# A graph layer on one core: maxima of turned tiles and clearing of sums moved to ScalarE, the additions at segment ends moved away from their products, 75 columns and 16 single lines a chunk

## The chip, the core and the metric

The kernel runs on one core of a Trainium2 chip. The metric is the device time of one execution in microseconds (us). A core has five engines with a queue of instructions each: TensorE (PE), VectorE (DVE), ScalarE (ACT), GpSimd (POOL) and SyncE (SP). They run side by side and wait for each other by semaphores only.

## The reference

There are 12,500 nodes of 48 numbers and 400,000 edges of 32 numbers, sorted by their target `dst`; the sources `src` are in no order.

```python
h = jnp.maximum(_layernorm(x, axis=-1), 0.0)
tmp = jnp.concatenate([h[dst], h[src], edge_attr], axis=1)
msg = jax.nn.relu(tmp @ W1 + b1) @ W2 + b2
return x + jax.ops.segment_sum(msg, dst, num_segments=12500)
```

## The kernel before

A first stage of about 100 us (`node_tables`) makes two tables of the nodes: `tab_a` (h times the target's part of W1, with b1) and `tab_b` (h times the source's part), both in device memory with one line of 128 numbers a node, and `bt`, which is `tab_b` turned, with a column a node, in SBUF.

Then `windows` walks through the edges. A chunk `c` is 1,024 edges, in eight tiles of 128; there are 391. As the edges are sorted, the targets of a chunk lie in a window of 80 nodes. For each chunk:

- SP loads 80 lines of `tab_a` (`rhs`), the edges' attributes and targets (`lhs`, `row`). DVE makes `lhs` one-hot rows out of the targets (L463) and `hot`, the same as columns (L469). PE multiplies `lhs` with `rhs` into `pre` (L481): targets' part and attributes' part in one product of a tile.
- The sources' part of a tile comes in one of three ways. POOL fetches 128 lines of `tab_b` with an indirect DMA into `gb` (L452), and DVE adds them to `pre` (L517). Or the tile is "turned": DVE and ACT copy 128 single columns of `bt` into a tile `gt`, one instruction a column (L393), and PE turns and adds that to `pre` (L491). Or it is a "single" tile: SP fetches 128 lines, one DMA a line (L425), into `gr`, and DVE adds them (L515).
- DVE takes the maximum with zero: of gathered and single tiles in place in `hid` (L530), of turned tiles from `pre` to `hid` (L532).
- PE multiplies `hid` with `hot` into `p_g` (L541), and counts with `ones` (L546); DVE adds `p_g` to `seg` (L560).

A table `PARTS` says how many columns are copied per chunk: 71 by DVE in four parts, 80 by ACT in five. With 151 columns per chunk 458 tiles are turned (`tiles_of`: 389 * 151 // 128), with 12 single lines 36 tiles are single (389 * 12 // 128), and 3125 - 458 - 36 = 2631 are left for POOL. Each part's node numbers are loaded into the engine's registers first (`numbers`, L358, a TENSOR_LOAD in the engine's own queue).

Twelve chunks are a segment, kept in one of two buffers `seg` of 1,024 nodes. After the last chunk of a segment DVE clears the other buffer (L576) and copies what overlaps (L578). In the next two iterations PE multiplies half of `seg` each with W2 and b2 into `p_f` (L586, L587), DVE adds it to `xseg` (L588), and SP stores.

The order of the work is written by hand (`manual_schedule`): in iteration `c` stand `prepare(c)`, `before(c - 1)`, `fold(c - 2)`, `turned(c - 1)`, then the segment's sum, `gathered(c - 1)`, `hidden(c - 1)` and `add(c - 2)`, with DVE's parts of columns in between and ACT's at the end. PE's last product into `pre` waits for the fetched lines. POOL may run up to seven chunks ahead (`gp` has eight buffers; `paced` ties a fetch to DVE's work of seven chunks earlier). ACT writes ahead into the `gt` buffers, of which there are five.

Of the kernel before, what the change touches and what calls it, by code (L numbers as in the profile page):

```python
# [8 lines left out]
F32 = mybir.dt.float32  # L9
I32 = mybir.dt.int32  # L10
# [6 lines left out]
P = 128  # L17
# [5 lines left out]
T = 8  # L23
# [12 lines left out]
BLK = 512  # L36
STORE = 2
NOUT = NPAD + L
# [16 lines left out]
PARTS = (  # L55
    (True, 0, 19, 1),
    (True, 19, 20, 20),
    (True, 39, 16, 40),
    (True, 55, 16, 56),
    (False, 71, 16, 72),  # L60
    (False, 87, 16, 88),
    (False, 103, 16, 104),
    (False, 119, 16, 120),
    (False, 135, 16, 136),
)
PART = sum(n for _, _, n, _ in PARTS)
BASE = 152
DVE_PARTS = sum(dve for dve, *_ in PARTS)

BT0 = 16512  # L70
SEG0 = 130848
SEG_SIZE = 8 * L


SEG, NEXT, SEG2 = 153, 154, 155
PLACE0 = 156
SINGLE = 12
SINGLE_AT = 160
WIDTH = 172
SLOTS = (NCH + 2 + P - 1) // P  # L80
MOST = 32


# [195 lines left out]
def windows(nc, tc, gp, bt, ident, idx, x_t, tab_a, tab_b, dst, edge_t, w1, w2s, b2s, out_t):  # L279
# [3 lines left out]
    with ExitStack() as es:  # L283
# [3 lines left out]
        one = es.enter_context(tc.tile_pool(name="wone", bufs=1))  # L287
        ld = es.enter_context(tc.tile_pool(name="ld", bufs=3))
        gtp = es.enter_context(tc.tile_pool(name="gtp", bufs=5))
        wp = es.enter_context(tc.tile_pool(name="wp", bufs=3))  # L290
        grp = es.enter_context(tc.tile_pool(name="grp", bufs=3))
# [25 lines left out]
        for a, b in ((place, SEG2), (NEXT, SEG)):  # L317
# [36 lines left out]
        def numbers(c, at, n, engine):  # L354

            got = []
            for k in range(0, n, MOST):
                got += nc.values_load_multi_w_load_instructions(  # L358
                    last[c % P : c % P + 1, c // P, at + k : at + min(k + MOST, n)],
                    engines=[engine], min_val=0, max_val=1 << 23,  # L360
                    skip_runtime_bounds_check_because="numbers of nodes, and what is made of them",
                )[1]
            return got
# [66 lines left out]
        def prepare(c):  # L430
# [8 lines left out]
            )  # L439
            lhs = ld.tile([P, CE], F32, name="lhs")  # L440
            nc.sync.dma_start(lhs[W:K, : n * P], edge_t[:, at : at + n * P])
# [66 lines left out]
        def gathered(c):  # L508

            s = st[c]  # L510
            s["h"] = h = wp.tile([P, T, HID], F32, name="hid")
# [5 lines left out]
            added = nc.vector.tensor_add(to, of, rows)  # L517
            after(added.ins, s["behind"], "the rows are there when the product is")
            for fetch in s["fetches"]:
                tc.declare_no_dep(  # L520
                    added.ins, fetch, reason="the product that is waited for waits for the rows"
                )
            mark(added, 1.0)
            spans[c], marks[:] = list(marks), []

        def hidden(c):

            s = st[c]
            of = apart(c, s["h"], False)
            mark(nc.vector.tensor_scalar(of, of, 0.0, None, op0=ALU.max), 0.55)  # L530
            if turned_at(c):
                nc.vector.tensor_scalar(  # L532
                    apart(c, s["h"], True), apart(c, s["pre"], True), 0.0, None, op0=ALU.max
                )

# [28 lines left out]
        def segment_load(g):  # L564
# [4 lines left out]
            nc.sync.dma_start(xs[g][:, :n], x_t[:, bass.ds(node(first), n)])  # L569

        def segment_next(g):

            old, new = segs[g % 2], segs[(g + 1) % 2]
            if g > 0:
                for k in range(2):
                    nc.vector.memset(new[:, k, W:], 0.0)  # L576
# [5 lines left out]
        def segment_sum(g, k, n):  # L582

            seg, s = segs[g % 2], slice(k * BLK, k * BLK + n)
            p_f = ps_f.tile([D, BLK], F32, name="p_f")
            nc.tensor.matmul(p_f[:, :n], w2s, seg[:, 0, s], start=True, stop=False)  # L586
            nc.tensor.matmul(p_f[:, :n], b2s[:1, :], seg[:1, 1, s], start=False, stop=True)  # L587
            nc.vector.tensor_add(xs[g][:, s], xs[g][:, s], p_f[:, :n])  # L588

# [4 lines left out]
        with tc.manual_schedule():  # L594
            for c in range(NCH + 2):
                if c < NCH:
                    prepare(c)
                    singles(c)
                if c >= NCH:
                    load(c, 0)  # L600
                    columns(c, 0)
                load(c, 1)
                columns(c, 1)
                if 0 <= c - 1 < NCH:
                    before(c - 1)
# [160 lines left out]
def tile_gnn_preln(  # L766
# [52 lines left out]
    flag = const.tile([1, 1], I32, name="flag")  # L819
    last = const.tile([P, SLOTS, WIDTH], I32, name="last")  # L820

# [156 lines left out]
```

## Time and profile before

| | |
|---|---|
| three runs | 3528.13, 3527.61, 3518.28 us, median 3527.61 |
| the profiled execution | 3517.03 us, of which the span of the instructions is 3515.3 us |
| busy share of the span | DVE 92%, ACT 89%, POOL 76%, PE 74% |
| granted TensorE clock, mean | 0.781 |
| DMA engines, mean busy share | about a third after the first stage |

Busy time leaves out register loads, semaphores and the issue of DMAs. "Idle before" is the time in which the engine did nothing ahead of the instructions of a group, with the one that ended the wait behind the arrow; "issue" is a wait that no semaphore explains. "SPq", "DVEq" name the engine's sequencer, which issues DMAs and loads registers.

### The profile page before, as it was taken

How to read it: one execution, taken by the hardware profiler on the slowest of the kernel's cores; microseconds unless marked ns; L12 is line 12 of the kernel's file. 1: busy time of each engine (PE TensorE's matmuls, PEld its weight loads, DVE VectorE, ACT ScalarE, POOL GpSimd, SP SyncE). 2: the span in 40 equal slices, each digit the busy share in tenths (PEclk: the TensorE clock that was granted, in tenths of full speed). 3: DMA queues.
4: the chain of work that ended last, by engine and by line, in shares of the span. 5: the costliest groups of instructions: out<-in, count | busy, mean ns of one | idle time of the engine just before them, and what ended most of it. 6: DMA issues, size and time to landing. Idle time of an engine off the chain costs nothing.

```text
span 3515.3 us, 119801 instructions
## 1 busy us (share of the span) xinstructions
PE 2616.9 (74%) x17111; PEld 2351.3 (67%) x17111; DVE 3234.7 (92%) x30218; ACT 3123.3 (89%) x31115; POOL 2660.5 (76%) x2658
## 2 busy tenths in 40 slices
PE   8677777777777776777777777777777777777777
PEld 5567666666676666666666766666667666676666
DVE  6799999999999999999999999999999999999997
ACT  5899998999998899989999899899999999898893
POOL 5777777777777777777777777777777777777775
PEclk9777777778777778778877787777777778778777
DMA  5533333333333333333333333333333333333332
GB/s 198 169 98 99 95 94 95 93 93 104 96 96 93 93 95 98 97 95 94 96 94 94 100 96 94 95 93 94 103 96 95 93 93 96 97 100 97 92 94 68
DMA packets 197238, 349.02 MB, mean 99 GB/s; under 512 B 67762, under 2 KB 104516, under 8 KB 195156
## 3 DMA queue, kind: packets, MB, share of 16 engines
q0 software_dynamic: 84224, 172.62, 19.3%
q1 hardware_dynamic: 111952, 168.56, 16.1%
q14 instruction: 658, 5.39, 0.5%
q8 instruction: 144, 2.36, 0.3%
q10 hardware_dynamic: 260, 0.10, 0.0%
HBM read 321.55 MB, written 22.07 MB: 98 GB/s over the span
## 4 chain that ended last, share of the span: by engine, by line
DVE 75%; PE 10%; ACT 5%; issue 4%; DVEq 3%; ACTq 0%; DMA 0%; SPq 0%
DVE gt L393 40%; DVE hid L517 9%; DVE hot L469 7%; DVE lhs L463 6%; DVE hid L530 6%; ACT gt L393 5%; PE p_g L541 4%; DVEq L358 3%; DVE seg L560 2%; DVE hid L532 2%; PE p_f L586 2%; PE p_f L587 2%; DVE xseg L588 1%; PE pre L491 1%; DVE seg L576 1%
## 5 line engine op out<-in xcount | busy, mean ns | idle before, releaser
L393 ACT COPY gt<-bt 128x1 f32 x31040 | 3076.9, 187 | 298.9 <-PE pre L491 195.5
L452 POOL DMA_INDIRECT gb<-tab_b,srci x2631 | 2639.0, 1003 | 821.8 <-issue 373.3
L393 DVE COPY gt<-bt 128x1 f32 x27584 | 1813.3, 143 | 147.6 <-issue 98.3
L541 PE MATMUL p_g<-hot,hid 128*128 128x80 f32 x6250 | 1069.5, 342 | 839.5 <-DVE hid L530 838.5
L541 PEld LDWEIGHTS p_g<-hot,hid 128*128 128x128 f32 x6250 | 1001.1, 251 | 913.1 <-DVE hid L530 903.5
L481 PEld LDWEIGHTS pre<-rhs,lhs 112*128 112x128 f32 x6250 | 963.0, 243 | 92.1 <-issue 91.6
L481 PE MATMUL pre<-rhs,lhs 112*128 112x128 f32 x6250 | 989.7, 326 | 20.0 <-DMA lhs<-in_edge_t 17.4
L517 DVE TENSOR_TENSOR hid<-pre,gb 128x896 f32<-128x896 f32 (+2 forms) x391 | 408.0, 1044 | 0.0
L469 DVE TENSOR_TENSOR hot<-wnum,rel 128x640 f32<-128x640 f32 x391 | 318.2, 814 | 0.0
L463 DVE TENSOR_SCALAR lhs<-row,bw 80x1024 f32<-80x1024 int16 x391 | 289.7, 741 | 10.0 <-DMA row<-in_dst 10.0
L491 PE MATMUL pre<-ident,gt 128*128 128x128 f32 x916 | 271.3, 404 | 17.5 <-issue 12.1
L530 DVE TENSOR_SCALAR hid<-hid 128x896 f32<-128x896 f32 (+2 forms) x391 | 244.9, 626 | 0.1
L546 PE MATMUL p_g<-hot,ones 128*128 128x80 bf16 x3125 | 240.0, 238 | 0.0
L546 PEld LDWEIGHTS <-ones 128*128 128x128 bf16 x3125 | 239.9, 132 | 0.0
L491 PEld LDWEIGHTS pre<-ident,gt 128*128 128x128 f32 x916 | 193.1, 269 | 20.1 <-issue 14.3
L560 DVE TENSOR_TENSOR seg<-seg,p_g 128x160 f32 x391 | 122.4, 313 | 7.5 <-issue 3.5
L532 DVE TENSOR_SCALAR hid<-pre 128x128 f32<-128x128 f32 (+1 forms) x389 | 118.0, 303 | 0.0
L588 DVE TENSOR_TENSOR xseg<-xseg,p_f 48x512 f32<-48x512 f32 (+1 forms) x67 | 45.0, 672 | 63.9 <-PE p_f L587 63.8
L586 PE MATMUL p_f<-seg,w2s 128*48 128x512 f32 (+1 forms) x134 | 102.8, 861 | 0.4 <-DVE seg L560 0.4
L587 PE MATMUL p_f<-seg,b2s 1*48 1x512 f32 (+1 forms) x134 | 90.7, 763 | 0.0
L587 PEld LDWEIGHTS p_f<-seg,b2s 1*48 1x48 f32 x134 | 12.6, 137 | 84.3 <-issue 83.1
L576 DVE MEMSET seg<- 128x944 f32 x64 | 54.1, 845 | 9.3
(67 smaller groups left out, 289.4 us busy)
## 6 DMA issues: line engine op xcount, KB each, us to landing
gr<-tab_b SPq DMA_DIRECT2D x4608, 0.5 KB
row<-in_dst SPq DMA_DIRECT2D x390, 160.0 KB
lhs<-in_edge_t SPq DMA_DIRECT2D x390, 128.0 KB
gb<-tab_b,srci POOLq DMA_INDIRECT x2631
rhs<-tab_a SPq DMA_DIRECT2D x391, 40.0 KB
xseg<-in_x_t SPq DMA_DIRECT2D x33, 192.0 KB
out_x<-xseg SPq DMA_DIRECT2D x33, 192.0 KB
tab_b<-tab SPq DMA_DIRECT2D x3, 1280.0 KB
```

The lines of the kernel that those rows point to most:

```text
L393: done = copy(gts[of][:, e : e + 1], bt8[:, bass.ds(at, 4)].bitcast(F32))
L452: fetch = nc.gpsimd.indirect_dma_start(out=gb[:, t, :], out_offset=None, in_=tab_b[:, :], in_offset=bass.IndirectOffsetOnAxis(ap=srci[:, c ...
L463: mark(nc.vector.tensor_scalar(lhs[:W, : n * P], row[:, : n * P], bw[:, c : c + 1], None, op0=ALU.is_equal,), 0.8)
L469: mark(nc.vector.tensor_tensor(hot[:, :n, :], wnum.unsqueeze(1).to_broadcast([P, n, W]), rel[:, c * T : c * T + n].unsqueeze(2).to_broadca ...
L481: s["behind"] = nc.tensor.matmul(pre[:, t, :], s["lhs"][:K, t * P : (t + 1) * P], s["rhs"][:K, :], start=True, stop=t not in turned_at(c), ...
L491: s["behind"] = nc.tensor.matmul(s["pre"][:, t, :], gts.pop(j), ident, start=False, stop=True).ins
L517: added = nc.vector.tensor_add(to, of, rows)
L530: mark(nc.vector.tensor_scalar(of, of, 0.0, None, op0=ALU.max), 0.55)
L532: nc.vector.tensor_scalar(apart(c, s["h"], True), apart(c, s["pre"], True), 0.0, None, op0=ALU.max)
L541: nc.tensor.matmul(p_g[:, 0, :], s["h"][:, t, :], s["hot"][:, t, :], start=t == 0, stop=t == n - 1)
L546: nc.tensor.matmul(p_g[:, 1, :], ones, high[:, t, 1::2], start=t == 0, stop=t == n - 1)
L560: mark(nc.vector.tensor_add(to, to, s["p_g"]), 0.25)
```

## The change

- `PARTS`: DVE copies 75 columns per chunk in parts of 15, 20, 20 and 20 (before 19, 20, 16 and 16), ACT 80 as before. 471 tiles are turned, 82 chunks have two of them (before 69).
- `SINGLE` is 16: 48 tiles are single. POOL fetches 3125 - 471 - 48 = 2606 tiles.
- The maxima of turned tiles are taken by ACT (`hidden_turned`), one iteration later than before, behind ACT's first part of columns. That part now stands ahead of PE's products of the iteration.
- The clearing of `seg` is done by ACT in the sixth iteration of the next segment (`segment_clear`), as a copy of a zero.
- The segment's products stand in the first and third iteration of a segment, their additions in the second and fourth, ahead of `gathered`; the store follows in the fifth. At the end of the program the last segment's additions and products follow each other.
- `lhs` and `hid` are three fixed buffers each; there are eight buffers `gt` instead of five.
- The table of numbers uses 16 of each 32 partitions, in seven columns of lines instead of four.

```diff
-STORE = 2
+STORE = 4
+CLEAR = 5
+HIDS = LOADS = 3
 PARTS = (
-    (True, 0, 19, 1),
-    (True, 19, 20, 20),
-    (True, 39, 16, 40),
-    (True, 55, 16, 56),
+    (True, 0, 15, 1),
+    (True, 15, 20, 16),
+    (True, 35, 20, 36),
+    (True, 55, 20, 56),
...
-SINGLE = 12
+SINGLE = 16
...
+HALF_ROWS = 16
+USED = P // 2
+LAST = (NCH + 2 + USED - 1) // USED
+def row_of(c):
+    group, row = divmod(c % USED, HALF_ROWS)
+    return 2 * HALF_ROWS * group + row, c // USED
...
-        gtp = es.enter_context(tc.tile_pool(name="gtp", bufs=5))
+        gtp = es.enter_context(tc.tile_pool(name="gtp", bufs=8))
...
+        lhss = [one.tile([P, CE], F32, name=f"lhs{k}") for k in range(LOADS)]
+        hids = [one.tile([P, T, HID], F32, name=f"hid{k}") for k in range(HIDS)]
...
         def hidden(c):
...
+        def hidden_turned(c):
             if turned_at(c):
-                nc.vector.tensor_scalar(
-                    apart(c, s["h"], True), apart(c, s["pre"], True), 0.0, None, op0=ALU.max
-                )
+                relus[c] = nc.scalar.activation(
+                    apart(c, st[c]["h"], True), apart(c, st[c]["pre"], True), AF.Relu
+                ).ins
...
+        def segment_clear(g, k):
+            new = segs[(g + 1) % 2][:, k, W:]
+            nc.scalar.copy(new, nothing.to_broadcast([P, L - W]))
...
-            if g > 0:
-                for k in range(2):
-                    nc.vector.memset(new[:, k, W:], 0.0)
...
+                g, k = group(c - 2)
+                if g > 0 and k in (1, 3):
+                    segment_sum(g - 1, k // 2, BLK)
+                load(c, DVE_PARTS)
+                columns(c, DVE_PARTS)
                 if 0 <= c - 1 < NCH:
                     before(c - 1)
                 if 0 <= c - 2 < NCH:
+                    hidden_turned(c - 2)
                     fold(c - 2)
                 if 0 <= c - 1 < NCH:
                     turned(c - 1)
-
-                g, k = group(c - 2)
+                if g > 0 and k in (0, 2):
+                    segment_product(g - 1, k // 2, BLK)
                 if k == GQ - 3 or c == NCH - 1:
                     segment_load(g)
-                if g > 0 and k < L // BLK:
-                    segment_sum(g - 1, k, BLK)
...
-                for part in range(DVE_PARTS, len(PARTS)):
+                for part in range(DVE_PARTS + 1, len(PARTS)):
                     load(c, part)
                     columns(c, part)
+                    if g > 0 and k == CLEAR and part >= len(PARTS) - 2:
+                        segment_clear(g, part - len(PARTS) + 2)
                 if c == NCH + 1:
+                    segment_sum(g - 1, 1, BLK)
+                    segment_store(g - 1, L)
+                    segment_product(g, 0, END_L)
                     segment_sum(g, 0, END_L)
                     segment_store(g, END_L)
```

The order in which the engines' instructions stand shows it at two places. On DVE, the second half of an ordinary chunk before, from the addition of the fetched lines (L517) to the one-hot rows of the next chunk (L463):

```order
L517 TENSOR_TENSOR hid<-pre,gb 128x896
L358 TENSOR_LOAD last
L393 COPY gt<-bt 128x1 x16
L530 TENSOR_SCALAR hid<-hid 128x896
L532 TENSOR_SCALAR hid<-pre 128x128
L358 TENSOR_LOAD last
L560 TENSOR_TENSOR seg_663<-seg_663,p_g 128x2x80
L393 COPY gt<-bt 128x1 x16
L463 TENSOR_SCALAR lhs<-row,bw 80x1024
```

The same half chunk in the changed kernel (L533, L553, L586 and L479 are the addition, the maximum, the addition of sums and the one-hot rows):

```order
L533 TENSOR_TENSOR hid_719<-pre,gb 128x896
L374 TENSOR_LOAD last
L409 COPY gt<-bt 128x1 x20
L553 TENSOR_SCALAR hid_719<-hid_719 128x896
L374 TENSOR_LOAD last
L586 TENSOR_TENSOR seg_663<-seg_663,p_g 128x2x80
L409 COPY gt<-bt 128x1 x20
L479 TENSOR_SCALAR lhs_715<-row,bw 80x1024
```

The maximum of the turned tile is gone from between the maximum in place and the register load, and both trains of copies, and with them the loads, are four longer.

On DVE at the end of a segment, before (L560 adds the last chunk's sums, L576 clears the other buffer, L578 copies the overlap with a register's offset):

```order
L530 TENSOR_SCALAR hid<-hid 128x896
L532 TENSOR_SCALAR hid<-pre 128x128
L358 TENSOR_LOAD last
L560 TENSOR_TENSOR seg_663<-seg_663,p_g 128x2x80
L576 MEMSET seg_664 128x944 x2
L358 TENSOR_LOAD last
L578 ISA
L578 COPY seg_664<-seg_663 128x2x80
L393 COPY gt<-bt 128x1 x16
```

The same place on DVE in the changed kernel (L553, L586 and L606 are the maximum, the addition and the copy of the overlap):

```order
L553 TENSOR_SCALAR hid_719<-hid_719 128x896
L374 TENSOR_LOAD last
L586 TENSOR_TENSOR seg_663<-seg_663,p_g 128x2x80
L374 TENSOR_LOAD last
L606 ISA
L606 COPY seg_664<-seg_663 128x2x80
L409 COPY gt<-bt 128x1 x20
```

Both clearings are gone from DVE, and the load of the offset follows the addition directly. On ACT the two clearings stand behind the last two parts of columns of another chunk, and a maximum stands behind the first part of every chunk that has a turned tile.

More of the change, by code (lines that the diff above doesn't have):

```diff
@@ L55 @@
 PARTS = (
-    (True, 0, 19, 1),
-    (True, 19, 20, 20),
-    (True, 39, 16, 40),
-    (True, 55, 16, 56),
[L60 to L64, printed above, removed]
+    (True, 0, 15, 1),
+    (True, 15, 20, 16),
+    (True, 35, 20, 36),
+    (True, 55, 20, 56),
+    (False, 75, 16, 76),
+    (False, 91, 16, 92),
+    (False, 107, 16, 108),
+    (False, 123, 16, 124),
+    (False, 139, 16, 140),
 )
 PART = sum(n for _, _, n, _ in PARTS)
-BASE = 152
+BASE = 156
 DVE_PARTS = sum(dve for dve, *_ in PARTS)
 BT0 = 16512
-SEG0 = 130848
+SEG0 = 133152
 SEG_SIZE = 8 * L
-SEG, NEXT, SEG2 = 153, 154, 155
-PLACE0 = 156
-SINGLE = 12
-SINGLE_AT = 160
-WIDTH = 172
+SEG, NEXT, SEG2 = 157, 158, 159
+PLACE0 = 160
+SINGLE = 16
+SINGLE_AT = 164
+WIDTH = 180
 SLOTS = (NCH + 2 + P - 1) // P
 MOST = 32
+HALF_ROWS = 16
[4 more added lines that the diff above has]
+    return 2 * HALF_ROWS * group + row, c // USED
 def tiles_of(first, part):
@@ L287, in windows @@
         one = es.enter_context(tc.tile_pool(name="wone", bufs=1))
-        ld = es.enter_context(tc.tile_pool(name="ld", bufs=3))
-        gtp = es.enter_context(tc.tile_pool(name="gtp", bufs=5))
-        wp = es.enter_context(tc.tile_pool(name="wp", bufs=3))
+        ld = es.enter_context(tc.tile_pool(name="ld", bufs=LOADS))
+        gtp = es.enter_context(tc.tile_pool(name="gtp", bufs=8))
+        wp = es.enter_context(tc.tile_pool(name="wp", bufs=HIDS))
         grp = es.enter_context(tc.tile_pool(name="grp", bufs=3))
@@ L326, in windows @@
         )
+        nothing = one.tile([P, 1], F32, name="nothing")
+        nc.vector.memset(nothing, 0.0)
         for seg in segs:
@@ L356, in numbers @@
             got = []
+            row, slot = row_of(c)
             for k in range(0, n, MOST):
                 got += nc.values_load_multi_w_load_instructions(
-                    last[c % P : c % P + 1, c // P, at + k : at + min(k + MOST, n)],
+                    last[row : row + 1, slot, at + k : at + min(k + MOST, n)],
                     engines=[engine], min_val=0, max_val=1 << 23,
@@ L439, in prepare @@
             )
-            lhs = ld.tile([P, CE], F32, name="lhs")
+            lhs = lhss[c % LOADS]
             nc.sync.dma_start(lhs[W:K, : n * P], edge_t[:, at : at + n * P])
@@ L510, in gathered @@
             s = st[c]
-            s["h"] = h = wp.tile([P, T, HID], F32, name="hid")
+            s["h"] = h = hids[c % HIDS]
             to, of, rows = apart(c, h, False), apart(c, s["pre"], False), apart(c, s["gb"], False)
@@ L522, in gathered @@
                 )
+            if c - HIDS in relus:
+                tc.declare_no_dep(
+                    added.ins, relus.pop(c - HIDS),
+                    reason="the products that read this buffer last waited for that maximum",
+                )
             mark(added, 1.0)
             spans[c], marks[:] = list(marks), []
+        relus = {}
         def hidden(c):
@@ L580, in segment_next, with segment_product, segment_sum @@
             )
-        def segment_sum(g, k, n):
+        out_of = {}
+        def segment_product(g, k, n):
             seg, s = segs[g % 2], slice(k * BLK, k * BLK + n)
-            p_f = ps_f.tile([D, BLK], F32, name="p_f")
+            out_of[g, k] = p_f = ps_f.tile([D, BLK], F32, name="p_f")
             nc.tensor.matmul(p_f[:, :n], w2s, seg[:, 0, s], start=True, stop=False)
             nc.tensor.matmul(p_f[:, :n], b2s[:1, :], seg[:1, 1, s], start=False, stop=True)
-            nc.vector.tensor_add(xs[g][:, s], xs[g][:, s], p_f[:, :n])
+        def segment_sum(g, k, n):
+            s = slice(k * BLK, k * BLK + n)
+            nc.vector.tensor_add(xs[g][:, s], xs[g][:, s], out_of.pop((g, k))[:, :n])
         def segment_store(g, n):
@@ L819, in tile_gnn_preln @@
     flag = const.tile([1, 1], I32, name="flag")
-    last = const.tile([P, SLOTS, WIDTH], I32, name="last")
+    last = const.tile([P, LAST, WIDTH], I32, name="last")
     ones = const.tile([P, P], BF16, name="ones")
@@ L924 @@
     by_tile = src.reshape(NT, P)
-    numbers = np.zeros((SLOTS * P, WIDTH), np.int32)
+    numbers = np.zeros((LAST * USED, WIDTH), np.int32)
     first = dst[::CE]
@@ L942 @@
     numbers[COLS : COLS + len(rows), SINGLE_AT : SINGLE_AT + SINGLE] = rows
-    last = np.ascontiguousarray(numbers.reshape(SLOTS, P, WIDTH).transpose(1, 0, 2))
+    last = np.zeros((P, LAST, WIDTH), np.int32)
+    for c, row in enumerate(numbers):
+        at, slot = row_of(c)
+        last[at, slot] = row
     arrays = {
```

## The prediction

> **What bounds the kernel now.** I read the groups by line first, then the waits of POOL alone, then the timeline at both ends of the stream of fetches, and last one chunk on DVE, row by row. From the groups:
>
> ```profile
> L393 ACT COPY gt<-bt 128x1 f32 x31040 | 3076.9, 187 | 298.9 <-PE pre L491 195.5 <-issue 64.4 <-DMA gb<-tab_b,srci 5.1
> L452 POOL DMA_INDIRECT gb<-tab_b,srci x2631 | 2639.0, 1003 | 821.8 <-issue 373.3 <-DVE gt L393 175.9 <-DMA gb<-tab_b,srci 123.9
> L393 DVE COPY gt<-bt 128x1 f32 x27584 | 1813.3, 143 | 147.6 <-issue 98.3 <-ACT gt L393 2.2
> L517 DVE TENSOR_TENSOR hid<-pre,gb 128x896 f32<-128x896 f32 x284 | 306.6, 1080 | 0.0
> ```
>
> DVE shows as the busiest engine (92%) and POOL looks idle for a quarter of the span. The waits of POOL say what that idle time is:
>
> ```profile
> POOL gb L452 <- issue: 373.3, 1224, 0.3
> POOL gb L452 <- DVE gt L393: 175.9, 577, 0.3
> POOL gb L452 <- DMA tab_b<-tab: 19.8, 1, 19.8
> ```
>
> No wait ahead of a fetch but the very first is longer than 0.3 us, whatever is named as its releaser, so it is a fixed gap and no wait. Now the ends, in the timeline:
>
> ```profile
> 50.87 0.96 POOL L452 DMA_INDIRECT gb<-tab_b,srci  x1 [19.76 <-DMA tab_b<-tab]
> 106.32 0.81 DVE L469 TENSOR_TENSOR hot<-wnum,rel 128x640 f32<-128x640 f32 x1
> 3490.68 1.07 DVE L517 TENSOR_TENSOR hid<-pre,gb 128x896 f32<-128x896 f32 x1
> 3491.01 0.94 POOL L452 DMA_INDIRECT gb<-tab_b,srci  x1 [0.30 <-DVE xseg L588]
> ```
>
> POOL fetches without a pause from 50.87 to 3491.95: 3441.1 us for 2631 fetches, 1.308 us each. It begins 55 us ahead of DVE's first `hot`; at the end DVE adds the lines of the last chunk but one while the last fetch runs. On the way DVE never stood still ahead of L517 (idle 0.0), so it ran at a pace of its own and used the lead up:
>
> ```profile
> L469 DVE TENSOR_TENSOR hot<-wnum,rel x391: 566/814/821, 106.3 to 3487.8; 128x640 f32<-128x640 f32 x195, 128x400 f32<-128x400 f32 x1
> ```
>
> 390 steps from 106.3 to 3487.8 are 8.671 us a chunk; POOL's are 3441.1 / 391 = 8.801. So two engines bound the kernel, and both come in at the end together: relieving one alone gives next to nothing. The end is the later of POOL's stream and DVE's 390 chunks, and a tail of 23.4 us (3515.3 - 3491.95).
>
> **POOL's part of the change.** 458 + 36 tiles that are not fetched become 471 + 48: 25 fetches fewer, 2606. What one is worth stands in the spread of their durations:
>
> ```profile
> L452 POOL DMA_INDIRECT gb<-tab_b,srci x2631: 940/945/1783, 50.9 to 3491.0; - x188
> 2044.95 1.53 POOL L452 DMA_INDIRECT gb<-tab_b,srci  x1 [0.30 <-issue]
> 2045.06 0.61 DVE L530 TENSOR_SCALAR hid<-hid 128x896 f32<-128x896 f32 x1
> 2003.70 0.94 POOL L452 DMA_INDIRECT gb<-tab_b,srci  x1 [0.30 <-issue]
> 2004.94 0.94 POOL L452 DMA_INDIRECT gb<-tab_b,srci  x1 [0.30 <-DVE hot L469]
> 2006.19 0.94 POOL L452 DMA_INDIRECT gb<-tab_b,srci  x1 [0.30 <-DVE gt L393]
> ```
>
> An undisturbed fetch takes 0.945 and the gap 0.305: 1.25 us. The mean of 1.003 holds another 0.058 each, 153 us in all, lost in fetches like the one of 1.53 us, which lies across a maximum in place. Those maxima and the one-hot rows (L463) stay as many as there are chunks, so I take the loss as fixed and a removed fetch at 1.25: 25 * 1.25 = 31.2 us (at the mean of 1.308 it would be 32.7). POOL starts behind the first stage's stores; the larger table of numbers (645 KB instead of 344) is loaded ahead of them on SP's queue, and at the 198 GB/s of the first of forty slices the 301 KB more are 1.5 us; I take 1.2.
>
> ```profile
> GB/s 198 169 98 99 95 94 95 93 93 104 96 96 93 93 95 98 97 95 94 96 94 94 100 96 94 95 93 94 103 96 95 93 93 96 97 100 97 92 94 68
> last<-in_src_last SPq DMA_DIRECT2D x1, 344.0 KB
> ```
>
> POOL's sum: -30 us.
>
> Four more copies of a column a chunk on DVE are 1,564 more instructions beside the fetches. The three fetches above from 2003.70 to 2006.19 ran beside copies for most of their time, and each took 0.94, so I cost that at nothing. The Trainium skill says it otherwise ("SBUF — State Buffer", section "Who interferes with whom"): a copy can enter a two-port mode, and then VectorE holds the port pair that it shares with GpSimd for its whole instruction. By that rule the copies would hold fetches up; here the rows of 0.94 speak against it for copies of one column, and the row of 1.53 agrees with it for the maximum in place.
>
> **DVE's part.** One chunk, and the loads of registers in it:
>
> ```profile
> 2044.09 1.04 DVE L393 COPY gt<-bt 128x1 f32 x16
> 2045.59 0.27 DVE L532 TENSOR_SCALAR hid<-pre 128x128 f32<-128x128 f32 x1
> 2045.79 0.32 DVE L560 TENSOR_TENSOR seg<-seg,p_g 128x160 f32 x1
> 2046.03 1.05 DVE L393 COPY gt<-bt 128x1 f32 x16
> 2047.00 0.74 DVE L463 TENSOR_SCALAR lhs<-row,bw 80x1024 f32<-80x1024 int16 x1
> 2047.89 1.24 DVE L393 COPY gt<-bt 128x1 f32 x19 [0.15 <-issue]
> L358 DVEq TENSOR_LOAD <-last x1: 1391/1391/1391, 2003.4 to 2003.4; - x1
> L358 DVEq TENSOR_LOAD <-last x1: 1141/1141/1141, 2007.4 to 2007.4; - x1
> ```
>
> - Four more copies: 16 step from 2046.03 to 2047.00, 0.061 each: +0.243.
> - The maximum L532 gone: its step is 2045.59 to 2045.79, 0.20, its group's mean duration 0.303 (below); I take 0.24.
> - Register loads. The load of 20 numbers takes 1.39 us, that of 16 takes 1.14, and it starts when about ten instructions are still ahead of it: the one at 2007.4 began with eight copies and two maxima to go. Behind L463 today 1.39 us lie against nine copies and L463 (0.55 + 0.74): the next copies start 0.15 late, where neighbours elsewhere overlap by 0.08. With 15 columns and the base, 16 numbers, this 0.23 goes. Behind the maximum in place it turns round: 20 numbers, 1.39 and 0.09 to resume, against nine copies and the step of L530 alone (0.55 + 0.53): 0.40 exposed. So the removed L532 is mostly replaced by a load that it covered. Net +0.17.
> - Segment ends:
>
> ```profile
> L532 DVE TENSOR_SCALAR hid<-pre 128x128 f32<-128x128 f32 (+1 forms) x389 | 118.0, 303 | 0.0
> L588 DVE TENSOR_TENSOR xseg<-xseg,p_f 48x512 f32<-48x512 f32 (+1 forms) x67 | 45.0, 672 | 63.9 <-PE p_f L587 63.8
> L576 DVE MEMSET seg<- 128x944 f32 x64 | 54.1, 845 | 9.3
> ```
>
> The clearings go (54.1 + 9.3), and so do the waits for the product, now an iteration old (63.8, less some 12 in the tail); the load of the offset, which the clearings covered, costs perhaps 0.3 at 32 places: -(63.4 + 52 - 10) / 391 = -0.27 a chunk. Twelve more additions of single tiles and the narrower L517 cancel.
>
> Sum: 8.671 + 0.243 - 0.24 + 0.17 - 0.27 = 8.57, between 8.47 (all of the idle 147.6 us ahead of the copies gone) and 8.67. To let POOL set the end, DVE must begin the last chunk 30 us earlier than at 3487.8: (3457 - 107) / 390 = 8.59. It just does; the 55 us of lead cover the way there.
>
> **ACT, PE and SP.** ACT's copies and their issue gaps are 3076.9 + 64.4 us for 388 chunks' worth (31040 / 80), 8.10 each; the 195.5 us behind PE are waits for a free `gt`. Added are a maximum of 128 or 256 columns and, per twelve chunks, two copies of 944:
>
> ```profile
> L214 ACT ACTIVATE ht<-p_t 96x256 f32<-96x256 f32 x3 | 1.1, 376 | 0.0
> L189 ACT ACTIVATE sq<-xs 128x960 f32<-128x960 f32 x3 | 3.0, 1003 | 8.6 <-DVE xs L184 8.6
> ```
>
> At most 0.38, likelier 0.28, and 2 * 1.0 / 12 = 0.17: 8.55. It fits beside 8.57, hardly. The fold on PE now waits for ACT's maximum, and behind it stand the ones, the turned product and so DVE's L517; ACT in turn can be no further ahead than about a chunk, since it needs the product of two chunks back. Eight `gt` cost nothing and, with that, bring nothing. The products at segment ends keep their place on PE and lose only their waiters. SP issues four more lines a chunk:
>
> ```profile
> 2000.48 0.32 SPq L436 DMA_DIRECT2D rhs<-tab_a  x1
> 2002.70 4.28 SPq L425 DMA_DIRECT2D gr<-tab_b  x12
> 2007.73 0.32 SPq L436 DMA_DIRECT2D rhs<-tab_a  x1
> ```
>
> One round is 7.25 us there, a line 0.36, so 7.25 + 4 * 0.36 = 8.7 at most. Part of the 7.25 may be waiting for `rhs` and `lhs`; I take 8.4. In the tail the product leaves the way of the last L517, and comes back behind the last fold: nothing.
>
> **Sum.** The profiled execution took 3517.03, the runs 3528.13, 3527.61 and 3518.28; the mean of the four is 3522.8, and the profile lies near the lower pair. Against the profile: 3517.0 - 30 = 3487; against the mean, which I use: 3493. A change of 0.3%, 10.6 us, is about what can be told from none here, so faster means under 3517.
>
> **The rivals.**
>
> 1. DVE falls short of 8.59, by the load that is now exposed or by waits for the fold: at 8.63 the end moves up by 0.04 * 390 = 16 us, to 3509; from 8.62 on it decides. For it: four engines within 0.2 us a chunk. Against: ordinary chunks have little else that changes.
> 2. Slower: ACT's maximum holds up the fold. If ACT needs 8.75 a chunk (its waits for PE's product coming on top of 8.55), everything behind goes at that pace: (8.75 - 8.59) * 390 = 62 us more, 3555. It decides from about 8.68, where it eats the whole gain.
> 3. The fetches lose less: DVE, once it waits for POOL's lines, keeps a fixed phase to the fetches, and the 153 us are not fixed. A fifth less over all would be 3463; it can go the other way too, which rival 1's time covers.
> 4. The copies hold fetches up after all, by their 0.061: 1,564 * 0.061 = 95 us, 3588. The rows of 0.94 are against it.
> 5. Fewer fetches bring nothing since POOL waits elsewhere: excluded as long as its gaps stay 0.3.
>
> **Chances.** The forecast 0.52 (its own range 3480 to 3505), rival 1 0.20 (half of it under 3517), rival 3 0.16, rival 2 0.10, rival 4 0.02. Faster: 0.52 + 0.16 + 0.10 = 0.78; the same 0.10 (the other half of rival 1), slower 0.12. The range leaves out the far halves of rivals 2, 3 and 4: 3458 to 3528.
>
> **What would show it.** Right: 2606 fetches of about 1.0 us with gaps of 0.3 to the end, and an idle time ahead of the addition of the fetched lines that now ends on PE or a fetch; no idle ahead of the additions at segment ends; some 0.3 us ahead of the addition of sums in every chunk that ends on "issue". Wrong: gaps on POOL that grow, PE's fold waiting for ACT's maximum for more than a few us in all, or SP's lines landing late ahead of L463.

## The result, and the profile after

The changed kernel takes 3559.45 us (median of 4 runs, 3552.89 to 3569.53), the kernel before on the same chip 3522.95 (4 runs): ratio 1.0107, 95% interval 1.0074 to 1.0139, so 37 us slower. The profiled execution took 3557.15 with a span of 3555.1. In some of the experiments below the kernel before itself took 4400 to 4500 us, and the traces taken beside it show hundreds of microseconds of idle time on "issue" on ACT and DVE (891 and 724 us in the kernel with 71 columns and 12 lines); such a run is compared only with the kernel before that ran beside it.

The groups of the changed kernel that answer to those shown of before:

```profile
L409 ACT COPY gt<-bt 128x1 f32 x31113 | 3077.5, 187 | 201.0 <-issue 179.0
L468 POOL DMA_INDIRECT gb<-tab_b,srci x2606 | 2574.5, 988 | 880.9 <-issue 564.9
L409 DVE COPY gt<-bt 128x1 f32 x29175 | 1909.5, 143 | 124.5 <-issue 104.3
L533 DVE TENSOR_TENSOR hid<-pre,gb 128x896 f32<-128x896 f32 (+2 forms) x391 | 405.0, 1036 | 14.5 <-PE pre L507 13.8
L586 DVE TENSOR_TENSOR seg<-seg,p_g 128x160 f32 x391 | 125.9, 322 | 132.6 <-issue 129.2
L479 DVE TENSOR_SCALAR lhs<-row,bw 80x1024 f32<-80x1024 int16 x391 | 305.0, 780 | 10.6 <-DMA row<-in_dst 10.6
L622 DVE TENSOR_TENSOR xseg<-xseg,p_f 48x512 f32<-48x512 f32 (+1 forms) x67 | 44.7, 667 | 4.1 <-PE p_f L617 4.1
```

The 25 fetches are gone and a fetch is a little shorter (988 ns for 1003). The waits at segment ends are gone too (4.1 us for 63.8). New is the idle time ahead of the addition of sums, 132.6 us. Now POOL's waits:

```profile
POOL gb L468 <- issue: 564.9, 1848, 0.9
POOL gb L468 <- DVE gt L409: 157.1, 458, 2.0
POOL gb L468 <- DVE hid L533: 52.1, 128, 2.8
```

The longest is 2.8 us, where before only the very first was over 0.3: POOL no longer runs without a pause. It waits for DVE, to whose work of seven chunks earlier `paced` ties it, and whose addition of a chunk's lines (L533) frees their buffer. The rows of the two engines' streams, and POOL at the end:

```profile
L485 DVE TENSOR_TENSOR hot<-wnum,rel x391: 562/811/820, 106.7 to 3533.7; 128x640 f32<-128x640 f32 x195, 128x400 f32<-128x400 f32 x1
L468 POOL DMA_INDIRECT gb<-tab_b,srci x2606: 938/944/1512, 52.1 to 3485.0; - x187
3481.52 1.20 POOL L468 DMA_INDIRECT gb<-tab_b,srci  x1 [0.79 <-DVE gt L409]
3483.19 0.94 POOL L468 DMA_INDIRECT gb<-tab_b,srci  x1 [0.46 <-DVE gt L409]
```

DVE's pace is (3533.7 - 106.7) / 390 = 8.787 us a chunk, 0.116 longer than before. POOL's last fetch starts 49 us ahead of DVE's last `hot`: its lead of 55 us, which before was used up on the way, is still there. DVE alone sets the end (3533.7 and a tail of 21.4 are the span), and the chain that ended last says so:

```profile
DVE 81%; issue 7%; PE 5%; DVEq 3%; SPq 1%; DMA 0%
```

The fold on PE waits for the same instruction as before, DVE's maximum in place (the first line is of before, the second of after); no wait of the fold for ACT stands among PE's waits:

```profile
PE p_g L541 <- DVE hid L530: 838.5, 352, 5.5
PE p_g L567 <- DVE hid L553: 840.9, 341, 5.8
```

One chunk of DVE, with the load of the numbers for the last part of copies:

```profile
2005.53 1.08 DVE L533 TENSOR_TENSOR hid<-pre,gb 128x896 f32<-128x896 f32 x1
2006.52 1.30 DVE L409 COPY gt<-bt 128x1 f32 x20
2007.73 0.62 DVE L553 TENSOR_SCALAR hid<-hid 128x896 f32<-128x896 f32 x1
2008.86 0.32 DVE L586 TENSOR_TENSOR seg<-seg,p_g 128x160 f32 x1 [0.51 <-issue]
2009.10 1.29 DVE L409 COPY gt<-bt 128x1 f32 x20
2010.32 0.74 DVE L479 TENSOR_SCALAR lhs<-row,bw 80x1024 f32<-80x1024 int16 x1
2010.97 0.99 DVE L409 COPY gt<-bt 128x1 f32 x15
2011.88 0.81 DVE L485 TENSOR_TENSOR hot<-wnum,rel 128x640 f32<-128x640 f32 x1
2012.89 1.24 DVE L409 COPY gt<-bt 128x1 f32 x19 [0.19 <-issue]
L374 DVEq TENSOR_LOAD <-last x1: 1360/1360/1360, 2007.4 to 2007.4; - x1
```

The load starts at 2007.4 and takes 1.36; the addition comes 0.09 behind its end, at 2008.86, though the maximum was done at 2008.35. Where DVE used to run the maximum of the turned tile under a load of 16 numbers, it now stands still under one of 20.

Over the 213 chunks that hold no work of a segment's end, the period rose from 8.282 to 8.583 us; the rest of this section works with means over these chunks of both traces (an idle of -0.08 is the usual overlap of neighbours):

| place on DVE | before | after | difference | as forecast |
|---|---|---|---|---|
| four more copies | | | +0.24 | +0.24 |
| maximum of the turned tile gone (step 0.22) | | | -0.22 | -0.24 |
| idle behind the one-hot rows | 0.203 | -0.058 | -0.26 | -0.23 |
| idle ahead of the addition of sums | -0.060 | 0.338 | +0.40 | +0.40 |
| idle behind `hot` | 0.148 | 0.223 | +0.075 | 0 |
| idle behind the addition of the lines | -0.071 | -0.031 | +0.04 | 0 |
| one-hot rows' own duration | 0.740 | 0.782 | +0.04 | 0 |

Over all chunks the mean is 0.39 us above that of these chunks before (8.671 - 8.282) and 0.20 after (8.787 - 8.583): the work at segment ends costs 0.19 us a chunk less, and not 0.27. The copy of the overlap, whose offset's load now follows the addition directly, makes its chunk 9.31 us (from one-hot rows to one-hot rows) where an ordinary one is 8.58.

### The profile page after: what moved, and what is told of

Read it like the earlier page. It is cut to its first block, busy times and chain, and to the rows that moved or that the text cites. A ratio compares the mean times of both kernels' runs of the same rounds, so it can differ in the third digit from the quotient of the medians.

```text
span 3555.1 us, 124692 instructions
## 1 busy us (share of the span) xinstructions
PE 2666.9 (75%) x17137; PEld 2388.2 (67%) x17137; DVE 3214.5 (90%) x31369; ACT 3248.9 (91%) x31641; POOL 2595.9 (73%) x2633
## 4 chain that ended last, share of the span: by engine, by line
DVE 81%; issue 7%; PE 5%; DVEq 3%; SPq 1%; DMA 0%
DVE gt L409 46%; DVE hid L533 10%; DVE hot L485 7%; DVE lhs L479 7%; DVE hid L553 6%; DVE seg L586 3%; DVEq L374 3%; PE p_g L567 2%; PE pre L497 1%; DVE xseg L622 1%; PE p_f L616 1%; PE p_f L617 1%; PE pre L507 0%; PE p_g L572 0%; SPq L441 0%
## 5 line engine op out<-in xcount | busy, mean ns | idle before, releaser
L468 POOL DMA_INDIRECT gb<-tab_b,srci x2606 | 2574.5, 988 | 880.9 <-issue 564.9
L409 DVE COPY gt<-bt 128x1 f32 x29175 | 1909.5, 143 | 124.5 <-issue 104.3
L567 PE MATMUL p_g<-hot,hid 128*128 128x80 f32 x6250 | 1099.6, 349 | 841.0 <-DVE hid L553 840.9
L567 PEld LDWEIGHTS p_g<-hot,hid 128*128 128x128 f32 x6250 | 1032.8, 258 | 908.4 <-DVE hid L553 902.2
L497 PEld LDWEIGHTS pre<-rhs,lhs 112*128 112x128 f32 x6250 | 951.3, 240 | 109.1 <-issue 91.4
L533 DVE TENSOR_TENSOR hid<-pre,gb 128x896 f32<-128x896 f32 (+2 forms) x391 | 405.0, 1036 | 14.5 <-PE pre L507 13.8
L479 DVE TENSOR_SCALAR lhs<-row,bw 80x1024 f32<-80x1024 int16 x391 | 305.0, 780 | 10.6 <-DMA row<-in_dst 10.6
L586 DVE TENSOR_TENSOR seg<-seg,p_g 128x160 f32 x391 | 125.9, 322 | 132.6 <-issue 129.2
L553 DVE TENSOR_SCALAR hid<-hid 128x896 f32<-128x896 f32 (+2 forms) x391 | 242.6, 620 | 0.1
L558 ACT ACTIVATE hid<-pre 128x128 f32<-128x128 f32 (+1 forms) x389 | 112.8, 290 | 43.8 <-DVE hid L533 40.8
L600 ACT COPY seg<-nothing 128x944 f32<-128x944 f32 x64 | 62.2, 972 | 0.0
```

Source lines behind the costliest of these rows:

```text
L409: done = copy(gts[of][:, e : e + 1], bt8[:, bass.ds(at, 4)].bitcast(F32))
L468: fetch = nc.gpsimd.indirect_dma_start(out=gb[:, t, :], out_offset=None, in_=tab_b[:, :], in_offset=bass.IndirectOffsetOnAxis(ap=srci[:, c ...
L479: mark(nc.vector.tensor_scalar(lhs[:W, : n * P], row[:, : n * P], bw[:, c : c + 1], None, op0=ALU.is_equal,), 0.8)
L497: s["behind"] = nc.tensor.matmul(pre[:, t, :], s["lhs"][:K, t * P : (t + 1) * P], s["rhs"][:K, :], start=True, stop=t not in turned_at(c), ...
L567: nc.tensor.matmul(p_g[:, 0, :], s["h"][:, t, :], s["hot"][:, t, :], start=t == 0, stop=t == n - 1)
L586: mark(nc.vector.tensor_add(to, to, s["p_g"]), 0.25)
```

## The experiments

The theories: A, DVE falls behind by its loads of registers (20 numbers where 16 were) and copies, so the 75 columns are the cost; B, the work given to ACT (maxima, clearing) holds up the fold and with it DVE; C, added after the first runs, SP with 16 single lines a chunk is the next bound behind DVE. In later expectations D stands for the four copies themselves, apart from their loads.

**Everything kept, but 71 columns and 12 lines** (run e3b; parts of 19, 20, 16, 16 as before the change; the moves to ACT and at segment ends stay).

```
-    (True, 0, 15, 1),
-    (True, 15, 20, 16),
-    (True, 35, 20, 36),
-    (True, 55, 20, 56),
+    (True, 0, 19, 1),
+    (True, 19, 20, 20),
+    (True, 39, 16, 40),
+    (True, 55, 16, 56),
...
-SINGLE = 16
+SINGLE = 12
```

> The same kernel as e3_71_12: the changed kernel with 71 columns on DVE (19, 20, 16, 16) and 12 single lines. Theory A: DVE needs about 8.4 us a chunk, POOL's 2631 fetches set the end, about 3515 us (3500 to 3525). Theory B: 3540 us or more.

Measured: 3487.45 us (3485.81 to 3491.33) against 3520.12, ratio 0.9911 [0.9894, 0.9928]. It beats both kernels, and is 13 us under the range that A gave. Its streams and waits:

```profile
L485 DVE TENSOR_TENSOR hot<-wnum,rel x391: 574/814/820, 106.4 to 3455.1; 128x640 f32<-128x640 f32 x195, 128x400 f32<-128x400 f32 x1
L468 POOL DMA_INDIRECT gb<-tab_b,srci x2631: 940/944/1517, 52.2 to 3463.8; - x188
POOL gb L468 <- issue: 412.9, 1354, 0.3
PE pre L507 <- DMA gb<-tab_b,srci: 204.1, 111, 4.0
DVE hid L533 <- PE pre L507: 65.4, 60, 5.1
SPq L452 <- PE pre L497: 340.6, 132, 8.3
SPq L626 <- DVE xseg L622: 274.4, 33, 38.3
```

POOL's gaps are 0.3 to the end; its last fetch now comes behind DVE's last `hot`, PE waits for fetched lines and DVE for PE. That is what the forecast described, with POOL alone setting the end, only that it comes without the 75 columns. The 2631 fetches end 27 us earlier than before because they take 0.992 us on average instead of 1.003. With all of ACT's new work in it, it refutes B as the cause. The moves alone are worth 33 us, so the columns and lines cost 3559 - 3487 = 72.

**The maxima of turned tiles back on DVE** (run e2b; 75 columns kept).

```
             mark(nc.vector.tensor_scalar(of, of, 0.0, None, op0=ALU.max), 0.55)
-
-        def hidden_turned(c):
-
             if turned_at(c):
-                relus[c] = nc.scalar.activation(
-                    apart(c, st[c]["h"], True), apart(c, st[c]["pre"], True), AF.Relu
-                ).ins
+                nc.vector.tensor_scalar(
+                    apart(c, s["h"], True), apart(c, s["pre"], True), 0.0, None, op0=ALU.max
+                )
...
-                    hidden_turned(c - 2)
```

> The same kernel as e2_max_on_dve: the changed kernel with the maxima of turned tiles back on DVE. Theory A: the maximum comes back into the gap that the load leaves, 3540 to 3570 us. Theory B: the fold no longer waits for ACT, under 3520 us.

Measured: 3580.95 us, ratio 1.0176 [1.0159, 1.0193], 11 us above A's range and far above B's. From its waits:

```profile
ACT seg L597 <- PE p_f L613: 211.8, 31, 10.1
DVE seg L583 <- issue: 33.7, 137, 0.5
```

The idle ahead of the addition falls from 129.2 us to 33.7, for the maximum lies over the load again, but an ordinary chunk comes to 8.613 us for 8.583: covering the load costs about as much as standing still. ACT has time to wait 211.8 us for the products at segment ends. B is refuted from this side as well.

**Shorter loads, all 75 copies** (run e8c; the loads of the two last DVE parts take 16 numbers; their last four copies use the first four registers again and copy the columns of other nodes, so the kernel leaves out some sources in turned tiles).

```
+                few = max(0, n - 4) if part in (2, 3) else n
-                nodes = numbers(c, at, n, engine) if n else []
+                nodes = numbers(c, at, few, engine) if few else []
+                nodes = (nodes + nodes[:4])[:n]
```

> The same kernel as e8_short_loads: all 75 copies a chunk on DVE, but 16 numbers instead of 20 loaded for each of the last two parts; the last four copies of those parts take the first four numbers again, so the sums of some turned tiles are left out. Theory A (the loads' length sets DVE's pace): exposed load behind the maximum 0.42 -> 0.15 us, POOL's 2606 fetches set the end, 3455 to 3490 us. Theory D (the four copies themselves cost the time): 3540 us or more. Between: both. Where the kernel before takes 4400 us or more, both theories leave it within 0.5% of that.

Measured: 3506.63 us (3504.63 to 3513.87), ratio 0.9959 [0.9943, 0.9975], against 1.0107 [1.0074, 1.0139] of the changed kernel. The time lies between A's range and D's. With every copy still there, the length of two loads alone gives back 52 of the 72 us. Its waits and POOL's stream (line numbers are two higher here):

```profile
DVE lhs L481 <- DMA row<-in_dst: 40.1, 46, 7.1
DVE seg L588 <- issue: 8.7, 31, 0.5
L470 POOL DMA_INDIRECT gb<-tab_b,srci x2606: 940/944/1496, 50.9 to 3480.0; - x187
```

The idle ahead of the addition is all but gone (8.7 us), and POOL's gaps are 0.3 again. But 2606 fetches end only 11 us earlier than 2631 did before (3480.9 for 3491.95), for they take 1.011 on average here. And DVE now waits for `row`, the rows of numbers that SP fetches: 40.1 us in 46 places.

**71 columns with 16 lines** (run e6c), to separate SP's lines from the columns.

```
-    (True, 0, 15, 1),
-    (True, 15, 20, 16),
-    (True, 35, 20, 36),
-    (True, 55, 20, 56),
+    (True, 0, 19, 1),
+    (True, 19, 20, 20),
+    (True, 39, 16, 40),
+    (True, 55, 16, 56),
...
 SINGLE = 16
```

> The same kernel as e6_71_16: 71 columns on DVE, 16 single lines. Theory A (only DVE's loads and copies slow the changed kernel): POOL's 2619 fetches set the end, 12 * 1.25 = 15 us under e3b, 3465 to 3480 us. Theory C (the four lines a chunk on SP cost something of their own: row comes late and DVE waits for it): no better than e3b, 3490 us or more, with tens of us of DVE's one-hot rows waiting for row. Where the kernel before takes 4400 us or more, both leave it within 1% of that.

Measured: 3504.40 us (3501.45 to 3508.28), ratio 0.9957 [0.9941, 0.9974]: four lines more on SP cost 17 us against the kernel with 12, and take 12 fetches from POOL for nothing. Its waits and DVE's stream:

```profile
DVE lhs L479 <- DMA row<-in_dst: 48.8, 58, 7.8
SPq L626 <- DVE xseg L622: 27.8, 1, 27.8
SPq L452 <- PE pre L497: 17.2, 12, 9.2
L485 DVE TENSOR_TENSOR hot<-wnum,rel x391: 575/815/822, 105.3 to 3480.7; 128x640 f32<-128x640 f32 x195, 128x400 f32<-128x400 f32 x1
```

SP's waits of 340.6 and 274.4 us with 12 lines are down to 17.2 and 27.8: SP is full. DVE goes at SP's pace, (3480.7 - 105.3) / 390 = 8.655. The chain that ended last names SP for 13%. Three rounds of SP in the changed kernel itself are as tight:

```profile
2000.43 5.15 SPq L441 DMA_DIRECT2D gr<-tab_b  x16
2006.34 0.32 SPq L452 DMA_DIRECT2D rhs<-tab_a  x1
2008.74 5.52 SPq L441 DMA_DIRECT2D gr<-tab_b  x16
2017.42 5.15 SPq L441 DMA_DIRECT2D gr<-tab_b  x16
2023.33 0.33 SPq L595 DMA_DIRECT2D xseg<-in_x_t  x1
2026.56 5.16 SPq L441 DMA_DIRECT2D gr<-tab_b  x16
```

8.31, 8.68 and 9.14 us from one round's lines to the next, the last with a segment's load in it. C holds: in e8c and e6c alike DVE's pace is SP's, 8.66, and SP hardly waits (19.6 and 26.3 us are its longest sums there behind the first stage in e8c). So of the 72 us some 17 are the way up to SP's pace, and what the two loads cost lies on top of it. What the four copies would cost by themselves, with SP out of the way, no run shows.

A wait for `row` costs DVE more than its line says. Where the one-hot rows waited for it in e6c, the load of the next part began with them, while elsewhere it began 0.41 us ahead of them on average; so DVE stood still another 0.77 us behind the one-hot rows, for 0.31 elsewhere.

**The order around the uncovered load.** First (run e4b) the addition of sums and the work at a segment's end ahead of the load:

```
                     hidden(c - 1)
-                load(c, 3)
                 if 0 <= c - 2 < NCH:
                     add(c - 2)
...
+                load(c, 3)
                 columns(c, 3)
```

> The same kernel as e4_add_first: the changed kernel with the addition of sums (and at segment ends the copy of the overlap) issued ahead of the last part's register load. Theory A (the register loads in DVE's queue set the pace): 0.42 us of exposed load a chunk becomes 0.18 or less, 3480 to 3520 us where the kernel before takes 3523. Theory B (ACT's new work holds the fold and DVE up): 3550 to 3570 us.

Measured: 3537.43 us, ratio 1.0052 [1.0035, 1.0069]: by the ratios (1.0107 to 1.0052) 19 us of the 37 come back, a time between A's range and B's. Ordinary chunks fall to 8.435, but the chunk with the overlap rises from 9.31 to 10.11:

```profile
1729.16 0.24 DVE L606 COPY seg<-seg 128x160 f32 x1
1730.62 1.30 DVE L409 COPY gt<-bt 128x1 f32 x20 [1.22 <-issue]
L374 DVEq TENSOR_LOAD <-last x1: 1359/1359/1359, 1729.2 to 1729.2; - x1
```

The load of the last part now starts with the copy of the overlap and has nothing else over it: 1.30 us of idle time on average behind that copy, where the changed kernel has none. The load of the offset is covered here (0.03 us of idle time ahead of the copy, for 0.27). Then (runs e7 and e7b) only the addition ahead, the segment's work behind:

```
+                if 0 <= c - 2 < NCH:
+                    add(c - 2)
                 load(c, 3)
...
-                    add(c - 2)
```

> The changed kernel with the addition of sums ahead of the last part's load, but the copy of the overlap at segment ends behind that load, so that its own load does not stand alone. Theory A: e4b's gain in ordinary chunks (0.15 us each) without its loss at segment ends (0.8 us in one chunk of twelve): DVE 8.65 us a chunk, 3500 to 3520 us. If ordinary chunks do not set the pace: as e4b, 3537 us.

> The changed kernel with the addition of sums ahead of the load of the last part, the work at segment ends where the changed kernel has it. The addition then covers 0.3 us of the load of 20 numbers, and the load at segment ends keeps its place: if the 0.34 us ahead of the addition are DVE's loss, ordinary chunks come to 8.43 to 8.5 and the time to 3515 to 3540; if the end is set elsewhere (SP's lines), it stays at 3550 to 3565.

Measured: 4432.97 us against 4421.78, ratio 1.0029 [1.0017, 1.0042], and 4495.64 against 4487.36, ratio 1.0025 [1.0011, 1.0039]. What this order does where the kernel before takes 3520 stays open.

**The last two parts 24 and 16** (run e5) instead of 20 and 20, so that the load behind the maximum is short:

```
-    (True, 35, 20, 36),
-    (True, 55, 20, 56),
+    (True, 35, 24, 36),
+    (True, 59, 16, 60),
```

> The changed kernel with DVE's last two parts of 24 and 16 columns instead of 20 and 20; every part's numbers begin and end on a multiple of four. Theory A: the last load shrinks to 16 numbers, 1.12 us, and its exposed time from 0.42 to 0.12 us a chunk, but the third load grows to 1.6 us against 1.51 of cover and shows some 0.15: 0.1 to 0.2 us a chunk less, 3490 to 3525 us. Theory B: 3550 to 3570 us.

Measured: 3572.75 us, ratio 1.0145 [1.0122, 1.0167]. The idle ahead of the addition falls to 0.07 us a chunk, but 0.255 appears behind the addition of the lines, where the load of 24 numbers now lies (1.61 us): ordinary chunks 8.62. The stall was moved, not removed. The time is near what B gave, but not for its reason.

**Parts of 17, 19, 24 and 15** (run e1), the first try at it:

```
-    (True, 0, 15, 1),
-    (True, 15, 20, 16),
-    (True, 35, 20, 36),
-    (True, 55, 20, 56),
+    (True, 0, 17, 1),
+    (True, 17, 19, 18),
+    (True, 36, 24, 37),
+    (True, 60, 15, 61),
```

> The changed kernel with DVE's 75 columns split 17, 19, 24, 15 instead of 15, 20, 20, 20; nothing else. Theory A (the register loads in DVE's own queue set its pace: 20 numbers behind the maximum in place stand uncovered, 129 us ahead of the addition of sums in all): 15 numbers there take about 1.08 us against about 1.09 of cover, the idle time ahead of the addition of sums falls from 0.34 to under 0.1 us a chunk, DVE needs about 8.4 us a chunk and runs into POOL's stream: about 3490 us (3475 to 3515). Theory B (ACT's new work holds the fold up, and with it DVE): the split matters nothing, 3550 to 3570 us.

Measured: 7223.67 us against 4478, ratio 1.6137 [1.61, 1.6174]; no theory had this. Its group of copies on DVE and two of its loads:

```profile
L409 DVE COPY gt<-bt 128x1 f32 x29175 | 1918.2, 144 | 2925.9 <-issue 2919.0 <-DMA gr<-tab_b 3.3
L374 DVEq TENSOR_LOAD <-last x1: 4275/4275/4275, 2009.0 to 2009.0; - x1
L374 DVEq TENSOR_LOAD <-last x1: 5369/5369/5369, 2014.1 to 2014.1; - x1
```

The copies are as long as ever; the loads of 19 and 24 numbers take 4.28 and 5.37 us. The three parts that start at the numbers 18, 37 and 61 are all slow, the one at 0 is not (1.57 for 18 numbers). The run shows by accident that a load's length goes straight into DVE's chunk.

**The columns and lines alone** (runs e9 and e9b): the kernel before with 75 columns and 16 lines.

> The kernel before with the 75 columns (15, 20, 20, 20) and 16 lines alone; maxima, clearing and segment ends stay as before. Theory A: +0.24 us of copies and about as much again or less of exposed loads a chunk, 8.75 to 9.0 us a chunk on DVE with all the cost of the segment ends: 3570 to 3630 us. Theory B (ACT's new work is what slows the changed kernel): 3520 us or less, as 25 fetches are saved.

> The kernel before with 75 copied columns (parts of 15, 20, 20, 20) and 16 single lines a chunk, and nothing else of the change. If the columns and lines are what costs and the moved operations are worth some 33 us by themselves (3520 against 3487 with 71 columns and 12 lines), this lies between 3570 and 3610, slower than the changed kernel, with POOL waiting on DVE in the second half. If the moved operations are the cost, it lies under 3520.

Measured: 4476.01 us against 4421.78, ratio 1.0126 [1.0109, 1.0143], and 4531.66 against 4487.36, 1.0119 [1.0092, 1.0147]. The columns and lines cost time without the moves as well; where the kernel before takes 3520 us, this kernel was not run. The other kernels that ran beside a kernel before of over 4400 us, with their expectations:

> The changed kernel with the columns and lines of before: 71 columns on DVE in parts of 19, 20, 16 and 16, 12 single lines; maxima and clearing on ACT, segment ends apart. Theory A: DVE needs about 8.4 us a chunk (four copies fewer, -0.24; the last load 16 numbers, -0.3; the load behind the one-hot rows 20 again, +0.26), but POOL has its 2631 fetches back and sets the end: about 3515 us (3500 to 3525). Theory B: ACT's work is all still there, 3540 us or more.

> The changed kernel with the maxima of turned tiles back on DVE, behind the maximum in place; clearing, segment ends, columns and lines as changed. Theory A: the maximum (0.22 us a step) comes back into a gap of 0.42 us that the load leaves, so the time hardly moves: 3540 to 3570 us, and the idle time ahead of the addition of sums falls to about 0.15 us a chunk. Theory B: the fold no longer waits for ACT, under 3520 us.

> The changed kernel with the addition of sums (and at segment ends the copy of the overlap) issued ahead of the last part's register load instead of behind it; same instructions, same sizes. Theory A: the load then lies against eight copies, the maximum and the addition (0.49 + 0.54 + 0.24 = 1.27 us against 1.45), so 0.42 of exposed time becomes 0.18, DVE needs about 8.5 us a chunk: 3480 to 3520 us. Theory B: 3550 to 3570 us.

> The changed kernel with 71 columns on DVE (19, 20, 16, 16) but 16 single lines kept. Theory A (the four columns and the longer loads slow DVE; with 71 columns POOL's fetches set the end, as in e3b at 3487): 2619 fetches instead of 2631, 12 * 1.25 = 15 us less, 3465 to 3480 us. Theory C (the four lines a chunk on SP are what slows it): no better than e3b, 3490 us or more.

> The changed kernel with all 75 copies a chunk on DVE, but only 16 numbers loaded for each of the last two parts instead of 20; the last four copies of those parts take the first four numbers again, so the sums of some turned tiles are left out. Theory A (the loads' length sets DVE's pace): exposed load behind the maximum 0.42 -> 0.15 us, DVE about 8.3 us in an ordinary chunk, POOL's 2606 fetches set the end: 3455 to 3490 us. If the four copies themselves or their writes cost the time: 3540 us or more.

> The same kernel as e6_71_16: 71 columns on DVE, 16 single lines. Theory A and D: POOL's 2619 fetches set the end, 3465 to 3480 us. Theory C (the four lines a chunk on SP are what slows it): no better than e3b, 3490 us or more.

> The same kernel as e8_short_loads: all 75 copies a chunk on DVE, but 16 numbers instead of 20 loaded for each of the last two parts; the last four copies of those parts take the first four numbers again, so the sums of some turned tiles are left out. Theory A (the loads' length sets DVE's pace): exposed load behind the maximum 0.42 -> 0.15 us, POOL's 2606 fetches set the end, 3455 to 3490 us. Theory D (the four copies themselves cost the time): 3540 us or more. Between: both.

| kernel | before, us | this, us | ratio |
|---|---|---|---|
| 71 columns, 12 lines (e3) | 4478 | 4495.14 | 1.0036 [1.0023, 1.005] |
| maxima back on DVE (e2) | 4478 | 4477.1 | 1.0002 [0.999, 1.0015] |
| addition and segment's end ahead of the load (e4) | 4478 | 4504.73 | 1.0055 [1.0035, 1.0075] |
| 71 columns, 16 lines (e6, e6b) | 4421.78, 4483.25 | 4445.06, 4507.78 | 1.0062 [1.0045, 1.0079], 1.0044 [1.0026, 1.0062] |
| short loads (e8, e8b) | 4421.78, 4483.25 | 4426.81, 4485.77 | 1.0014 [1.0002, 1.0025], 1.0014 [1.0001, 1.0027] |

They say little of the question: a chunk takes 11 us there, POOL pauses for DVE again and again (690.5 us in 737 waits behind DVE's copies in e3), and the shorter loads leave the time as it is (1.0014). What sets the time there stays open. The kernel that gains 0.9% otherwise loses 0.4% here.

## Why the prediction was wrong

- **The step that failed is DVE's sum**, "8.57, between 8.47 and 8.67": it is 8.787. The named parts came out nearly as worked out (the table above: the copies, the maximum, and the load turned round, -0.26 and +0.40 for -0.23 and +0.40). Missing are 0.075 behind `hot`, 0.04 behind the addition of the lines and 0.04 in the one-hot rows, and segment ends gave -0.19 where -0.27 was taken. Ordinary chunks grew by 0.30 where the terms give 0.17; these 0.13 and the 0.08 at segment ends are the 0.21 between the sum and the measurement. I held a load's cover fixed in all places but two. A load starts when seven to ten instructions are still ahead of it, so each of four loads meets other neighbours when the parts change: behind a part of 15 columns the load for the next part starts later against `hot`, with 7.6 instructions ahead of it on average and 9.2 before. Why the one-hot rows take longer stays open.
- **The decision point was right, the margin wrong.** Rival 1 says that DVE decides from 8.62 on and each 0.01 costs 4 us; 8.787 by it gives (8.787 - 8.59) * 390 = 77 us over the forecast, and the profile is 70 over its 3487. I priced that rival at 8.63. An upper bound of 8.67 stood on terms that had themselves no bounds, and the lower one is not what its words give either (147.6 us are 0.38 a chunk, of which 0.23 was already taken off: 8.42, not 8.47).
- **POOL's -30 could not act**, since POOL waits for DVE and its stream, though it ends at 3486, no longer sets the end. Where it could (e8c), 25 fetches fewer brought 11 us at the end of its stream, while e3b brought 27 with none fewer: the mean fetch is 1.011 in the one and 0.992 in the other, and a hundredth of a microsecond is 26 us over 2,600 fetches. Taking the lost 153 us as fixed was wrong in both directions; rival 3 had that mechanism. The traces, fetch by fetch, show what the loss depends on: before, a fetch that lies across neither a maximum in place, the one-hot rows nor a clearing takes at most 0.96 us, and the whole loss is in the others. Those across the one-hot rows average 1.10 us before, 1.05 in e3b and 1.20 in e8c; 18 that lay across the clearings took over 1 us, up to 1.78, and none of that kind is left. The table of numbers is 630 KB by the profile and not 645, and the 1.2 us taken for it are no more than the first fetch's start varies with the same table (52.1 here, 50.9 in e8c). It was wrong, too, that relieving one engine alone gives next to nothing: e3b relieves DVE alone, gains 33 us, and POOL's fetches get shorter with it.
- **SP**: "8.7 at most ... I take 8.4". The bound was the value, 8.66. It cost next to nothing in the changed kernel, which DVE holds at 8.787 (10.6 us of waits for `row`), but it is why the repair of the loads alone stops at 3507.
- **Rival 2** gave 3555, next to the result, by a mechanism that isn't there: the fold's waits name DVE's maximum in place in the changed kernel as before, and the two experiments on ACT's work refute it. A right number is no evidence for its story.
- **Rival 4**: the mean fetch is 988 ns beside 1,591 more copies on DVE, no longer than before. The Trainium skill ("SBUF — State Buffer", section "Who interferes with whom") lets copies hold up GpSimd's fetches through the shared ports; of copies of one column no trace here shows it. In the changed kernel 341 fetches have no neighbour on DVE but copies, and the longest of them took 0.954 us, where the rival's price would make the mean 0.037 longer.
- Right were the fetches' number, no idle at the additions at segment ends (4.1 us), and idle on "issue" ahead of the addition of sums in nearly every chunk (375 of 391). Of the signs of being wrong the first came: POOL's gaps grew, to 2.8 us.

The gain of the moves, 33 us, is real; it was spent twice over by four columns and four lines more, the very part that was to relieve POOL.

## What to carry to other kernels

When two engines share the bound, moving work from the one to the other needs the receiver's margin, in the same unit, with an error on every term: here the margin was 0.02 us a chunk and the error 0.2. A load of registers is an instruction of the engine that it feeds and hides only under what is already queued, so lengthening one or changing the order around it moves stalls in every chunk; look at what each load lies under, not at one place. Try the parts of such a change apart: the half that frees an engine was good alone.

## What was not expected of the hardware

- A load of 16, 20 and 24 numbers into DVE's registers takes 1.11, 1.36 and 1.61 us, about 0.06 us a number. One that starts at number 18, 37 or 61 of the row of numbers takes 0.22 to 0.23 us a number (4.28 for 19, 5.37 for 24, 3.39 for 15). Loads of a single number are left aside here. Every kernel holds one more case: the first part of all is loaded without the base ahead of it, so it starts at number 1 and not at 0. It takes 4.29 us for 19 numbers in the kernel before and 3.43 for 15 in the changed one, 0.23 a number (the first line is of before, the second of after):

```profile
L358 DVEq TENSOR_LOAD <-last x1: 4289/4289/4289, 108.2 to 108.2; - x1
L374 DVEq TENSOR_LOAD <-last x1: 3425/3425/3425, 108.5 to 108.5; - x1
```

So the start makes the difference and not the length: 24 numbers take 1.61 us from number 36 (e5) and 5.37 from 37 (e1). The starts that are fast are 0 and multiples of four (20, 36 and 60 are not multiples of eight), and 18, which is even, is slow: a multiple of four numbers is what all of them fit. Why it matters, no run shows.
- SP issues a single line in 5.15 / 16 = 0.32 us, and 16 of them with three larger loads and its own loads of registers fill a round of 8.3 to 9.1 us: an engine that only issues DMAs can be the bound.
